# Layers 2 and 3 of a graph-network stack cut into units, with TensorE's order over three neighbouring chunks fixed by hand

## Chip, cores, metric

One core of one Trainium2 chip. The metric is the time of one execution on the device, in microseconds (us); the median of several runs is quoted. A ratio is the mean time of one kernel's runs over the mean of the other kernel's runs of the same rounds, so it is not quite the ratio of the medians quoted beside it; its 95% interval stands in brackets.

## The reference, cut

Four layers over x of 128 x 64 tokens x 256 channels, all in 32-bit floats. The change touches the last two:

```python
# layer 2: h = relu(layernorm(x))
q, k, v = split(h @ Wqkv);  s = q k^T / sqrt(256) + adj, causal
x = x + softmax(s) @ v @ Wo
# layer 3: h = relu(layernorm(x))
q, k, v = heads(h @ W);     s = q k^T / sqrt(64), -inf where adj == 0   # 4 heads of 64
x = x + softmax(s) @ v
```

(Layer 0 is a graph convolution with two batch norms, layer 1 graph convolutions and LSTMs; they take the first 1899 us and are the same in every kernel here.)

## The kernel before

The 8192 tokens are 16 chunks of 512. Each chunk's layers 2 and 3 are four functions; PE is TensorE, DVE VectorE, ACT ScalarE, POOL GpSimd. A scheduling layer takes the instructions as recorded and decides each engine's order. In the comments and views, h is the normalised input of a layer, hT its transpose, nmr the last value of the norm that h waits for (minus the mean, times rstd), tc_e and tc_f the transposes of h for layers 2 and 3, tr2 and tr3 the transposes of the softmax weights, att their copies, and o2 and o3 the outputs.

```python
        def layer2_scores(c):                               # "A"
            layernorm_relu(h, xt, f"e{c}")                  # DVE statistics, POOL rstd, ACT four h
            to_channels(hT, h, f"e{c}")                     # PE tc_e, then DVE and ACT copy hT
            nc.scalar.copy(q[:, 0, :], project_t(0, hT, wqk_sb, ...))        # PE p_q
            nc.vector.tensor_copy(q[:, 1, :], project_t(1, hT, wqk_sb, ...))
            project_v(v, hT, wvo_sb, 0, f"2_{c}")           # PE v
            ...                                             # PE scores s2, DVE mask
            softmax(s, NJ, at, f"2_{c}")                    # DVE max, POOL subtract, ACT exp, DVE
        def layer2_out(c):                                  # "B"
            transposed(at, NJ, att, f"2_{c}")               # PE tr2, ACT copies att
            ...                                             # PE o2, DVE adds it to x
        def layer3_scores(c):                               # "C"
            layernorm_relu(h, xt, f"f{c}")
            to_channels(hT, h, f"f{c}")                     # PE tc_f
            ...                                             # PE p_q, p_k, v3, scores s3, softmax
        def layer3_out(c):                                  # "D"
            transposed(at, NJ * HEADS, att, f"3_{c}")       # PE tr3, ACT and DVE copy att
            ...                                             # PE o3: 16 matmuls with 64 columns

        for c in range(NCH + 2):
            if c < NCH:             layer2_scores(c)
            if c >= 2:              layer3_out(c - 2)
            if 1 <= c <= NCH:       layer3_scores(c - 1)
            if c < NCH:             layer2_out(c)
        # ... (cut: everything else; line breaks shortened)
```

Of the kernel before, what the change touches and what calls it, by code (L numbers as in the profile page):

```python
# [19 lines left out]
def kernel(  # L20
# [23 lines left out]
    B, T, D = x.shape  # L44
# [11 lines left out]
    NCH = B * T // CH  # L56
# [12 lines left out]
    def bank(name):  # L69
        return psum.tile([P, CH], F32, tag="ps", name=name)  # L70
# [97 lines left out]
    def to_channels(dst, src, name):  # L168

        for k in range(KD):  # L170
            ps = bank(f"tc{k}_{name}")
            for j in range(NJ):
                nc.tensor.transpose(ps[:, j * P : (j + 1) * P], src[:, j, k * P : (k + 1) * P], ident)
            if k % 2 == 0:
                nc.vector.tensor_copy(dst[:, k, :], ps)  # L175
            else:
                nc.scalar.copy(dst[:, k, :], ps)
# [220 lines left out]
    with tc.tile_pool(name="w2", bufs=1) as w2p, tc.tile_pool(name="l2", bufs=2) as l2:  # L398
# [33 lines left out]
        def project_v(dst, hT, w, first, name):  # L432
            for t in range(NJ // 2):
                ps = bank(f"v_{name}_{t}").rearrange("p (j d) -> p j d", d=D)
                for i in range(2):
                    j = 2 * t + i
                    for k in range(KD):
                        nc.tensor.matmul(ps[:, i, :], hT[:, k, j * P : (j + 1) * P],  # L438
                                         w[:, k, first : first + D], start=(k == 0),
                                         stop=(k == KD - 1))  # L440
                nc.scalar.copy(dst[:, 2 * t : 2 * t + 2, :], ps)

        def project_t(m, hT, w, name):
            ps = bank(f"p{m}_{name}")
            for k in range(KD):
                nc.tensor.matmul(ps, w[:, k, m * P : (m + 1) * P], hT[:, k, :],  # L446
                                 start=(k == 0), stop=(k == KD - 1))
            return ps
# [15 lines left out]
        def transposed(src, n, dst, name):  # L464

            for b in range(n // NJ):
                ps = bank(f"tr_{name}_{b}")
                for j in range(NJ):
                    nc.tensor.transpose(ps[:, j * P : (j + 1) * P], src[:, b * NJ + j, :], ident)
                d = dst[:, b * NJ : (b + 1) * NJ, :].rearrange("p j n -> p (j n)")  # L470
                if b % 2 == 0:
                    nc.scalar.copy(d, ps)  # L472
                else:
                    nc.vector.tensor_copy(d, ps)



        parts = {}

        def layer2_scores(c):  # L480
            xt = xs[c]
            h = l2.tile([P, NJ, D], F32, tag="h", name=f"h2_{c}")
            layernorm_relu(h, xt, f"e{c}")
            hT = l2.tile([P, KD, CH], F32, tag="hT", name=f"hT2_{c}")
            to_channels(hT, h, f"e{c}")
            q = l2.tile([P, KD, CH], F32, tag="q", name=f"q2_{c}")
            nc.scalar.copy(q[:, 0, :], project_t(0, hT, wqk_sb, f"q2_{c}"))
            nc.vector.tensor_copy(q[:, 1, :], project_t(1, hT, wqk_sb, f"q2_{c}"))
            v = l2.tile([P, NJ, D], F32, tag="v", name=f"v2_{c}")
            project_v(v, hT, wvo_sb, 0, f"2_{c}")  # L490
            ps = bank(f"s2_{c}")[:, : NJ * T].rearrange("p (j t) -> p j t", t=T)
            for j in range(NJ):
                for e in range(2):
                    t = slice((2 * j + e) * T, (2 * j + e + 1) * T)
                    for k in range(KD):
                        nc.tensor.matmul(ps[e * T : (e + 1) * T, j, :], q[:, k, t], hT[:, k, t],
                                         start=(k == 0), stop=(k == KD - 1))
            s = l2.tile([P, NJ, T], F32, tag="s2", name=f"s2_{c}")
            nc.vector.scalar_tensor_tensor(s, ps, float(D) ** -0.5,
                                           mask2[:, None, :].to_broadcast([P, NJ, T]),  # L500
                                           op0=OP.mult, op1=OP.add)
            at = at2[c % 2]
            softmax(s, NJ, at, f"2_{c}")
            parts[2, c] = at, v

        def layer2_out(c):
            xt = xs[c]
            at, v = parts.pop((2, c))
            att = l2.tile([P, NJ, P], F32, tag="att2", name=f"att2_{c}")
            transposed(at, NJ, att, f"2_{c}")  # L510
            for t in range(NJ // 2):
                ps = bank(f"o2_{c}_{t}").rearrange("p (j d) -> p j d", d=D)
                for i in range(2):
                    nc.tensor.matmul(ps[:, i, :], att[:, 2 * t + i, :], v[:, 2 * t + i, :],
                                     start=True, stop=True)
                nc.vector.tensor_add(xt[:, 2 * t : 2 * t + 2, :], xt[:, 2 * t : 2 * t + 2, :], ps)

        def layer3_scores(c):
            xt = xs[c]
            h = l2.tile([P, NJ, D], F32, tag="h", name=f"h3_{c}")  # L520
            layernorm_relu(h, xt, f"f{c}")
            hT = l2.tile([P, KD, CH], F32, tag="hT", name=f"hT3_{c}")
            to_channels(hT, h, f"f{c}")
            q = l2.tile([P, KD, CH], F32, tag="q", name=f"q3_{c}")
            kk = k3[c % 2]
            for m in range(KD):
                nc.scalar.copy(q[:, m, :], project_t(m, hT, w3_sb, f"q3_{c}"))
                ps = project_t(KD + m, hT, w3_sb, f"k3_{c}").rearrange("p (b t) -> p b t", t=T)
                for e in range(2):
                    r = slice(e * HD, (e + 1) * HD)  # L530
                    nc.vector.tensor_copy(kk[r, m, :, e, :], ps[r])  # L531
            v = l2.tile([P, NJ, D], F32, tag="v", name=f"v3_{c}")
            project_v(v, hT, w3_sb, 2 * D, f"3_{c}")
            s = l2.tile([P, NJ * HEADS, T], F32, tag="s3", name=f"s3_{c}")
            for g in range(NJ // 2):
                ps = bank(f"s3_{c}_{g}").rearrange("p (j f) -> p j f", j=2)
                for i in range(2):
                    for e in range(2):
                        b = 2 * (2 * g + i) + e
                        for m in range(KD):  # L540
                            nc.tensor.matmul(
                                ps[e * T : (e + 1) * T, i, m * 2 * T : (m + 1) * 2 * T],
                                q[:, m, b * T : (b + 1) * T],
                                kk[:, m, b].rearrange("p h t -> p (h t)"),
                                start=True, stop=True)
                n = 2 * HEADS
                nc.vector.scalar_tensor_tensor(
                    s[:, g * n : (g + 1) * n, :], ps.rearrange("p j (h t) -> p (j h) t", t=T),
                    float(HD) ** -0.5, mask3[:, None, :].to_broadcast([P, n, T]),
                    op0=OP.mult, op1=OP.add)  # L550
            at = at3[c % 2]
            softmax(s, NJ * HEADS, at, f"3_{c}")
            parts[3, c] = at, v

        def layer3_out(c):
            xt = xs[c]
            at, v = parts.pop((3, c))
            att = l2.tile([P, NJ * HEADS, P], F32, tag="att3", name=f"att3_{c}")
            transposed(at, NJ * HEADS, att, f"3_{c}")
            o = l2.tile([P, NJ, D], F32, tag="o", name=f"o_{c}")  # L560
            for t in range(NJ // 2):
                ps = bank(f"o3_{c}_{t}").rearrange("p (j d) -> p j d", d=D)
                for i in range(2):
                    j = 2 * t + i
                    for hd in range(HEADS):
                        f = slice(hd * HD, (hd + 1) * HD)
                        nc.tensor.matmul(ps[:, i, f], att[:, j * HEADS + hd, :], v[:, j, f],  # L567
                                         start=True, stop=True)
                nc.vector.tensor_add(o[:, 2 * t : 2 * t + 2, :], xt[:, 2 * t : 2 * t + 2, :], ps)
            nc.sync.dma_start(outr[c], o)  # L570

        for c in range(NCH + 2):
            if c < NCH:
                layer2_scores(c)
            if c >= 2:
                layer3_out(c - 2)
            if 1 <= c <= NCH:
                layer3_scores(c - 1)
            if c < NCH:
                layer2_out(c)  # L580


# [44 lines left out]
```

## Time and profile before

| | before |
|---|---|
| median (4 runs) | 2522.52 us (2521.32 to 2523.38) |
| rounds of layers 2 and 3 | 14 from 1950.08 to 2465.89 us, 36.84 us each |
| granted TensorE clock in them | 0.92 |
| TensorE at half clock | 5.6 us a round |

A *round* runs from the end of one chunk's layer-3 scores (s3) to the next. The clock is full or half in these records, so a granted clock of 0.92 (0.924 before rounding) means that 2 x (1 - 0.924) of the time is at half. In the rounds of this trace it is at half for 3.41, 6.83 or 10.24 us at a time, and these stretches begin whole steps of 3.4133 us apart, within 0.02 us; such a step is called a *window* below. From the page's groups of instructions (line, engine, operation, tiles, shapes, count; busy us, mean ns; idle time before and what ended it), layer 3's output:

```profile
L567 PE MATMUL o<-v,att 128*128 128x64 f32 x512 | 77.1, 322 | 26.5 <-ACT att L472 26.5
```

In a round at full clock these 32 entries take 3.6 us, that is 0.11 us each from start to start; the mean duration cannot be read as a cost per matmul, as matmuls overlap.

### The profile page before, as it was taken

To read this page: it belongs to the slowest core of one execution; us is meant where nothing else is said; L and a number is where in the kernel's file an instruction comes from. 1 tells how busy PE (TensorE), PEld (TensorE's weight loads), DVE (VectorE), ACT (ScalarE), POOL (GpSimd) and SP (SyncE) were. 2 spreads that over 40 slices of the span, in tenths; PEclk is the share of its full clock that TensorE was granted. 3 is DMA by queue.
4 is the path that set the end of the run, shared out by engine and by line. 5 is a ranking of instruction groups with operands and counts; after the bars stand their busy time and mean duration, and the time that the engine had idled before them with its cause. 6 is when DMAs were issued, how large, how long until landed. Compare 5 with 4: busy or idle time off the path is not lost.

```text
span 2518.0 us, 22830 instructions
## 1 busy us (share of the span) xinstructions
PE 2293.2 (91%) x9181; PEld 1485.8 (59%) x9181; DVE 897.6 (36%) x1892; ACT 825.6 (33%) x1479; POOL 178.7 (7%) x226
## 2 busy tenths in 40 slices
PE   6989699989989989989989989998997999989996
PEld 3544255854754764764674575575575666666665
DVE  5644322222232232231232232233223555555554
ACT  4544232323323323323323333233333323333331
POOL 2100100000010010010000000000002111111110
PEclk9999899989999999999999999999998898899998
DMA  3100400000000000000000000000000000000000
GB/s 94 59 0 1 150 14 1 1 17 1 1 17 0 1 17 0 1 17 1 1 9 9 1 9 9 0 1 1 0 1 30 16 10 18 17 9 18 17 17 18
DMA packets 30122, 37.78 MB, mean 15 GB/s; under 512 B 1856, under 2 KB 27456, under 8 KB 30016
## 3 DMA queue, kind: packets, MB, share of 16 engines
q1 hardware_dynamic: 27600, 27.89, 3.5%
q0 software_dynamic: 2256, 8.40, 0.9%
q8 instruction: 72, 1.18, 0.2%
q14 instruction: 34, 0.28, 0.0%
q10 hardware_dynamic: 160, 0.03, 0.0%
HBM read 27.93 MB, written 8.39 MB: 14 GB/s over the span
## 4 chain that ended last, share of the span: by engine, by line
PE 78%; DVE 10%; POOL 4%; ACT 3%; issue 2%; DMA 2%; SPq 0%; POOLq 0%; ACTq 0%; DVEq 0%
PE g L345 31%; PE g L352 16%; PE z L250 4%; PE o L567 3%; PE z L234 3%; PE p_q L446 3%; PE agg_b L163 2%; PE v L438 2%; PE u L318 2%; PE v L309 2%; PE p_k L446 2%; DMA xt<-in_x_dram 2%; DVE at L462 2%; ACT h L153 1%; PE agg_c L163 1%
## 5 line engine op out<-in xcount | busy, mean ns | idle before, releaser
L345 PE MATMUL g<-hT,wih 128*128 128x256 f32 (+2 forms) x2496 | 818.7, 483 | 3.8 <-ACT gate L368 3.8
L345 PEld LDWEIGHTS g<-hT,wih 128*128 128x128 f32 x2496 | 468.2, 188 | 334.2 <-issue 192.5
L358 ACT ACTIVATE gate<-g,bias 128x256 f32<-128x256 f32 (+2 forms) x624 | 350.6, 562 | 747.9 <-PE g L352 616.8
L352 PE MATMUL g<-hs,whh 128*128 128x256 f32 (+2 forms) x1536 | 435.8, 437 | 0.0
L352 PEld LDWEIGHTS g<-hs,whh 128*128 128x128 f32 x1536 | 291.3, 190 | 132.2 <-issue 62.0
L362 DVE TENSOR_TENSOR cell<-cell,gate 128x256 f32<-128x256 f32 (+2 forms) x96 | 48.7, 508 | 466.6 <-ACT gate L358 466.6
L163 PE MATMUL agg_b<-adjt_bd,h 128*128 128x128 f32 x256 | 61.4, 431 | 85.3 <-ACT h L153 85.3
L392 POOL COPY hn<-hT 128x512 f32<-128x512 f32 x32 | 36.3, 1210 | 1335.7 <-DVE hT L374 1335.7
L367 DVE TENSOR_TENSOR cell<-gate,gate 128x512 f32<-128x512 f32 (+2 forms) x80 | 48.2, 602 | 224.0 <-ACT gate L358 224.0
L234 PE MATMUL z<-agg,w_sb 128*128 128x512 f32 x256 | 116.3, 608 | 8.1 <-DVE agg L227 6.9
L250 PE MATMUL z<-h,w_sb 128*128 128x512 f32 x256 | 111.6, 599 | 5.0 <-ACT h L245 5.0
L163 PEld LDWEIGHTS agg_b<-adjt_bd,h 128*128 128x128 f32 x256 | 57.3, 314 | 90.0 <-ACT h L153 89.6
L368 ACT ACTIVATE gate<-cell 128x256 f32<-128x256 f32 (+2 forms) x176 | 89.9, 511 | 50.0 <-DVE cell L367 41.0
L567 PE MATMUL o<-v,att 128*128 128x64 f32 x512 | 77.1, 322 | 26.5 <-ACT att L472 26.5
L374 DVE TENSOR_TENSOR hT<-gate,gate 128x512 f32<-128x512 f32 (+2 forms) x80 | 48.1, 601 | 127.2 <-PE g L345 100.5
L567 PEld LDWEIGHTS o<-v,att 128*128 128x128 f32 x512 | 74.7, 235 | 29.9 <-ACT att L472 29.8
L250 PEld LDWEIGHTS z<-h,w_sb 128*128 128x128 f32 x256 | 49.2, 193 | 67.4 <-issue 57.2
L234 PEld LDWEIGHTS z<-agg,w_sb 128*128 128x128 f32 x256 | 48.0, 193 | 66.2 <-issue 47.8
L531 DVE COPY k<-p_k 64x512 f32<-64x512 f32 x64 | 44.1, 689 | 102.9 <-PE p_k L446 102.5
L446 PE MATMUL p_q<-hT,w_sb 128*128 128x512 f32 x128 | 73.9, 708 | 2.3 <-DVE hT L175 2.3
L153 ACT ACTIVATE h<-xs,nmr_b,rstd_b 128x256 f32<-128x256 f32 x64 | 33.2, 588 | 127.0 <-DVE nmr_b L151 127.0
L371 DVE TENSOR_TENSOR hs<-gate,gate 128x256 f32<-128x256 f32 (+2 forms) x96 | 47.8, 497 | 72.8 <-ACT gate L368 44.6
(151 smaller groups left out, 2406.2 us busy)
## 6 DMA issues: line engine op xcount, KB each, us to landing
xt<-in_x_dram SPq DMA_DIRECT2D x32, 512.0 KB, 3.9
out_dram<-o SPq DMA_DIRECT2D x16, 512.0 KB, 2.9
wih<-in_wih_t_dram POOLq DMA_DIRECT2D x4, 1024.0 KB, 13.1
whh<-in_whh_t_dram POOLq DMA_DIRECT2D x3, 1024.0 KB, 17.9
w_sb<-in_w_dram SPq DMA_DIRECT2D x1, 768.0 KB, 4.4
wqkv_sb<-in_wqkv_dram SPq DMA_DIRECT2D x1, 768.0 KB, 4.4
w_sb<-in_w1t_dram POOLq DMA_DIRECT2D x1, 512.0 KB, 4.6
w_sb<-in_w2t_dram POOLq DMA_DIRECT2D x1, 512.0 KB, 5.7
```

Of the source, the lines that this page charges most:

```text
L153: nc.scalar.activation(dst[:, j, :], src[:, j, :], AF.Relu, bias=nmr[:, j : j + 1], scale=rstd[:, j : j + 1])
L163: nc.tensor.matmul(ps[:, j * P : (j + 1) * P], src[:, j, k * P : (k + 1) * P], mat, start=True, stop=True)
L234: nc.tensor.matmul(ps, w1_sb[:, k, m * P : (m + 1) * P], agg[:, k, :], start=(k == 0), stop=(k == KD - 1))
L250: nc.tensor.matmul(ps, w2_sb[:, k, m * P : (m + 1) * P], h1[:, k, :], start=(k == 0), stop=(k == KH - 1))
L309: nc.tensor.matmul(ps, wg0_sb[:, k, m * P : (m + 1) * P], agg[:, k, :], start=False, stop=(k == KD - 1))
L318: nc.tensor.matmul(ps[:, i, :], v[:, k, j * P : (j + 1) * P], wg1_sb[:, k, :], start=(k == 0), stop=(k == KD - 1))
L345: nc.tensor.matmul(banks[q][:, :n].rearrange("p (j w e) -> p j w e", w=nw, e=2), wi[:, k, o], hv[:, k, :, cols, :], start=(k == 0), stop=( ...
L352: nc.tensor.matmul(banks[q][:, :n], wh[:, k, o], hs[:, k, :n], start=False, stop=(k == KD - 1))
L358: nc.scalar.activation(g[q], banks[q][:, :n], AF.Tanh if q == 2 else AF.Sigmoid, bias=bs[:, q * KD + c : q * KD + c + 1])
L368: nc.scalar.activation(g[2], cell[c], AF.Tanh)
L446: nc.tensor.matmul(ps, w[:, k, m * P : (m + 1) * P], hT[:, k, :], start=(k == 0), stop=(k == KD - 1))
L567: nc.tensor.matmul(ps[:, i, f], att[:, j * HEADS + hd, :], v[:, j, f], start=True, stop=True)
```

## The change

Intent: no engine's work changes; TensorE's waits between a transpose and the use of its copied result are to be filled with another chunk's work. The four functions become generators that stop after each unit, and a table fixes TensorE's order.

```diff
             to_channels(hT, h, f"e{c}")
+            yield
...(a yield after every unit: norm, q, v, scores; transposed weights, output)
-        for c in range(NCH + 2):
-            if c < NCH:
-                layer2_scores(c)
-            if c >= 2:
-                layer3_out(c - 2)
-            if 1 <= c <= NCH:
-                layer3_scores(c - 1)
-            if c < NCH:
-                layer2_out(c)
+        stages = {"A": layer2_scores, "B": layer2_out, "C": layer3_scores, "D": layer3_out}
+        ROUND = (("A", 0), ("A", 0), ("A", 0), ("D", -2), ("C", -1), ("D", -2), ("C", -1), ("B", 0),
+                 ("C", -1), ("C", -1), ("A", 1), ("B", 0))
...
+        with tc.manual_schedule(engines={mybir.EngineType.PE}):
+            unit("A", 0)
+            for c in range(NCH + 2):
+                for stage, d in ROUND:
+                    unit(stage, c + d)
```

More of the change, by code (lines that the diff above doesn't have):

```diff
@@ L488, in layer2_scores @@
             nc.vector.tensor_copy(q[:, 1, :], project_t(1, hT, wqk_sb, f"q2_{c}"))
+            yield
             v = l2.tile([P, NJ, D], F32, tag="v", name=f"v2_{c}")
             project_v(v, hT, wvo_sb, 0, f"2_{c}")
+            yield
             ps = bank(f"s2_{c}")[:, : NJ * T].rearrange("p (j t) -> p j t", t=T)
@@ L504, in layer2_scores @@
             parts[2, c] = at, v
+            yield
         def layer2_out(c):
@@ L510, in layer2_out @@
             transposed(at, NJ, att, f"2_{c}")
+            yield
             for t in range(NJ // 2):
@@ L516, in layer2_out @@
                 nc.vector.tensor_add(xt[:, 2 * t : 2 * t + 2, :], xt[:, 2 * t : 2 * t + 2, :], ps)
+            yield
         def layer3_scores(c):
@@ L523, in layer3_scores @@
             to_channels(hT, h, f"f{c}")
+            yield
             q = l2.tile([P, KD, CH], F32, tag="q", name=f"q3_{c}")
@@ L531, in layer3_scores @@
                     nc.vector.tensor_copy(kk[r, m, :, e, :], ps[r])
+            yield
             v = l2.tile([P, NJ, D], F32, tag="v", name=f"v3_{c}")
             project_v(v, hT, w3_sb, 2 * D, f"3_{c}")
+            yield
             s = l2.tile([P, NJ * HEADS, T], F32, tag="s3", name=f"s3_{c}")
@@ L553, in layer3_scores @@
             parts[3, c] = at, v
+            yield
         def layer3_out(c):
@@ L559, in layer3_out @@
             transposed(at, NJ * HEADS, att, f"3_{c}")
+            yield
             o = l2.tile([P, NJ, D], F32, tag="o", name=f"o_{c}")
@@ L570, in layer3_out, with unit @@
             nc.sync.dma_start(outr[c], o)
-        for c in range(NCH + 2):
-            if c < NCH:
-                layer2_scores(c)
-            if c >= 2:
-                layer3_out(c - 2)
-            if 1 <= c <= NCH:
-                layer3_scores(c - 1)
-            if c < NCH:
-                layer2_out(c)
+            yield
+        stages = {"A": layer2_scores, "B": layer2_out, "C": layer3_scores, "D": layer3_out}
+        ROUND = (("A", 0), ("A", 0), ("A", 0), ("D", -2), ("C", -1), ("D", -2), ("C", -1), ("B", 0),
+                 ("C", -1), ("C", -1), ("A", 1), ("B", 0))
+        units = {}
+        def unit(stage, c):
+            if 0 <= c < NCH:
+                if (stage, c) not in units:
+                    units[stage, c] = stages[stage](c)
+                next(units[stage, c])
+        with tc.manual_schedule(engines={mybir.EngineType.PE}):
[3 more added lines that the diff above has]
+                    unit(stage, c + d)
 def kernel(**inputs):
```

## The prediction

> **What bounds the kernel now.** I read the page's slices first, then what TensorE waited for, then one round of the last stage instruction by instruction. From the page of the kernel before:
>
> ```profile
> PE   6989699989989989989989989998997999989996
> PEclk9999899989999999999999999999998898899998
> ```
>
> TensorE (PE) is busy nearly everywhere, and the granted clock is worst in the last quarter (1899 to 2518 us), where layers 2 and 3 run: the only part that the diff touches. There 14 near-equal rounds run from 1950.08 to 2465.89, 515.8 us, 36.84 us each. PE's waits in that stretch:
>
> ```profile
> PE o L567 <- ACT att L472: 26.5, 14, 2.2
> PE p_q L446 <- DVE hT L175: 11.2, 17, 0.7
> PE o L514 <- ACT att L472: 9.4, 14, 0.7
> ```
>
> Only 47.1 us in 14 rounds, 3.4 us a round, is shown as waiting. The rest of the loss is clock. Two whole rounds and two stretches of the first, by the view of windows (the column after POOL busy is the granted clock):
>
> ```profile
> 2101.24:2138.60 37.36, 34.04 (x198) 24.50 (x196) 20.64 (x44) 12.22 (x22) 5.06 (x6) 0.91 0.05 15
> 2213.40:2248.06 34.66, 30.84 (x198) 22.21 (x197) 20.56 (x44) 12.22 (x22) 5.06 (x6) 1.00 0.05 16
> ...
> 2117.42:2120.83 3.41, 2.57 (x23) 2.57 (x24) 2.64 (x6) 3.06 (x7) 0.61 (x1) 1.00 0.00 0
> 2120.83:2127.66 6.83, 6.83 (x23) 4.95 (x23) 2.28 (x5) 0.69 (x2) 0.00 (x0) 0.50 0.23 77
> ```
>
> A round at full clock takes 34.66 us, one that falls to half clock for 6.83 us takes 37.36; the mean round loses 36.84 - 34.66 = 2.2 us to the clock. Now the middle of the round that starts at 2101.24 (end of layer 3's scores), all engines:
>
> ```profile
> 2113.22 1.20 PE L496 MATMUL s<-hT,q 128*64 128x64 f32 x32
> 2114.16 0.16 DVE L151 SCALAR_TENSOR_TENSOR nmr_f<-mv_f,rstd_f 128x4 f32<-128x4 f32 x1 [1.23 <-POOL rstd_f L81]
> 2114.35 1.97 PE L469 MATMUL tr<-ident,at 128*128 128x128 f32 x16
> 2114.41 1.09 ACT L153 ACTIVATE h<-xs,nmr_f,rstd_f 128x256 f32<-128x256 f32 x2 [2.17 <-DVE nmr_f L151]
> ...
> 2115.80 1.04 POOL L81 TENSOR_TENSOR rstd_e<-rstd_e,mhalf 128x4 f32<-128x4 f32 x1
> 2115.88 1.09 ACT L153 ACTIVATE h<-xs,nmr_f,rstd_f 128x256 f32<-128x256 f32 x2
> ...
> 2117.91 0.61 POOL L454 TENSOR_TENSOR s<-s,mx 128x256 f32<-128x256 f32 x1 [1.06 <-DVE mx L453]
> 2118.26 2.00 PE L567 MATMUL o<-v,att 128*128 128x64 f32 x16 [1.95 <-ACT att L472]
> 2118.56 0.42 ACT L455 ACTIVATE s<-s 128x256 f32<-128x256 f32 x1 [0.35 <-POOL s L454]
> ```
>
> The four normalised tiles h of layer 3's next chunk are ready only at 2116.97, 15.7 us into the round, and the exponential of layer 2's softmax starts 17.3 us in. That is no matter before, as PE comes to h only after layer 3's output, at 2122.83 (21.6 us in). Layer 3's output waits 1.95 us for its transposed weights, and the clock falls in its middle.
>
> [...] the granted-clock records of before fall to 0.5 for 3.41, 6.83 or 10.24 us. But windows need not be idle: one with 2.57 us of layer 3's output (64-column matmuls) lowered it, and three with nothing but that output at half clock did not restore it, while full windows of 512-column projections always did. [...] a window with only 1.8 us of transposes at 2226.6 did not lower the clock. [...]
>
> **The change part by part.** No instruction is added or removed; PE's order within a round becomes: h-transposes of layer 2 (tc_e), output of layer 2 (o2), p_q, v, scores s2, weight transposes of layer 3 (tr3), h-transposes of layer 3 (tc_f), output of layer 3 (o3), q/k projections, weight transposes of layer 2 (tr2), v3, scores s3. The scheduler re-orders the other engines to suit; I read their built order.
>
> Removed: tr2 followed at once by o2 (0.67 us wait) now has v3 and s3 between; tc_e followed at once by p_q (0.69) has o2 between; tc_f to q/k (0.5 at full clock) has o3 between; tr3 to o3 (1.95) has tc_f between. 3.8 us a round, the gain that was meant: 14 x 3.8 = 53 us, and more if the clock stays up.
>
> Added: tc_f comes right after tr3. When is h ready? I walk the round from t = 0 at the end of s3 with durations of the round shown (start-to-start where they overlap).
> - PE at full clock: tc_e 0.9, o2 1.83 to 2.73, p_q 3.53 to 6.26, v 3.55 to 9.81, s2 1.13 to 10.94, tr3 1.82 to **12.76**. Here PE wants h.
> - VectorE: mask of s3 to 0.80, hT copy (now ahead) to 1.52, row maximum to 2.77; GpSimd subtract 2.92 to 4.83; ScalarE exp to 5.94; VectorE sum 5.96, reciprocal, q copy, then the two 1.2 us products to 10.6; the last statistics of layer 3's norm end at 11.41 (they ended at 11.37 before). GpSimd's rstd takes 1.39 with its hand-overs, nmr at 12.96 (before: 12.92). So h's chain does not move, but its user comes 9 us earlier.
> - ScalarE's built order is h, h, weight copy, h, **exp of layer 2's softmax**, weight copy, h. The exp waits for GpSimd, which does rstd of layer 2's next norm first: VectorE reaches s2's mask at 13.83, ends the norm's statistics at 14.5, GpSimd rstd 14.66 to 16.02, subtract 16.1 to 16.7, exp to 17.2, copy to 17.6, the fourth h to **18.1**. In all middle rounds the built order is the same.
> - So PE stands from 12.76 to 18.1 (three transposes in between), o3 can start at 18.7 instead of 17.0. At full clock: 18.7 + o3 3.63 + q/k 6.97 + tr2 0.5 + v3 3.55 + s3 1.95 = **35.3 us**, against 34.66 before: the four short waits became one long one behind the same chain.
>
> Clock: PE does almost nothing for 5.3 us, so at least one window of 3.41 us is nearly empty in every round, and the clock falls between 15.0 and 18.4, before o3 starts. o3 does not restore it, so all of it runs at half: +3.6 us; the last transposes +0.5; then q/k until a window without o3 has passed, 2.6 to 6.0 us (mean 4.3, half lost: +2.1). Together +6.3: a round of about **41.6 us**, +4.8 over 36.84. Times 14: +67 us. The first round and the tail keep their waits (6.5 and 9.2 us behind the last softmaxes), +-2 us.
>
> **The rivals.** (1) What the author wants: all 3.8 us a round go, PE never stands, the clock stays at 1.00: a round of 30.9, 14 x -5.9 = -83 us, 2440 us. For it: every pair of transpose and use gets other work in between. Against it: h's first tile cannot be there before 13.2, and tr3 ends at 12.76. (2) The long wait is there, but the clock recovers during o3 or falls late, as in the trace's single-window cases: 35.3 + about 2.5 = 37.8, +1.0 a round, +14 us, 2537: the same. (3) Full clock throughout: 35.3, that is 14 x -1.5 = -21 us, 2502; it needs an empty window not to count, and the before-trace shows such windows lowering the clock every time. (4) Banks or transfers as a new bound: eight banks still suffice (tr3 4, tc_f 2, s2 and v one each before o3), and the output store takes 2.9 us of some 37; I give them nothing.
>
> **Range and chances.** The walk gives 2523 + 67 = 2590. I shade it to 2582, as (2) is half as likely as the main line. The low end, 2530, is rival (2); the high end, 2606, is +5.9 a round: four windows of half clock (13.65 us, half lost, where the main line has 12.6 us) and a chain 0.6 us longer. Slower by over 2% begins at 2573.5: 0.60. Same: 0.34, rivals (2) and (3) and a milder clock. Faster by over 2%: 0.06, if the walk misreads the chain.
>
> **What would show it.** Right: the waits named att and hT nearly vanish from PE's list, and one new line stands first, tc_f waiting for ScalarE's h, about 4 to 5 us a round; o3 takes about 7.2 us instead of 4.8; the granted clock in the stage falls from about 0.92 to near 0.83; rounds of 40 to 42 us. Wrong: the fourth h is earlier than 17 us into the round, or the clock is restored while o3 runs, or rounds are under 37 us.

(35.3 us of the walk and 6.3 us of clock make the 41.6 us. The clock's terms are estimates from windows of the trace before: three with 0.00, 0.22 and 0.56 us of matmuls (1895.55, 2468.99, 2496.29) were each followed by half clock; three with the output alone at half clock (1967.23, 2192.51, 2339.28) by half clock again, two with projections alone (2199.34, 2346.11) by full. The walk assumes that ScalarE and VectorE keep their built order. In the round at 2111.67 of the trace after they did: the norm (nmr_f) was done at 2124.34, yet ScalarE idled 1.25 us before the exponential and made the fourth h only behind it; VectorE idled 0.65 us for the next norm ahead of a copy of weights whose transposes had ended at 2124.42. TensorE's work stands there in the order of the table.)

## The result, and the profile after

| | before | after |
|---|---|---|
| median (4 runs each) | 2522.52 us | **2565.32 us** (2565.2 to 2567.33) |
| ratio | | 1.0172 [1.0154, 1.019] |
| mean of 14 rounds | 36.84 us | 40.06 us |
| half clock a round | 5.6 us | 12.7 us |

1.7% slower: within 2%, though clear of noise. The 14 rounds account for 14 x 3.22 = 45 us of the 45.3 us between the two profiled spans. The page's slices:

```profile
PE   6999699989989989989989989989989898988996
PEclk9999799999999999999999999999998888878888
```

TensorE looks as busy as before (91% of the span), which says nothing: its matmuls last longer at half clock (the output's 32 entries 6.7 us in the round below, 3.5 us at full clock in the first experiment). What TensorE waited for in layers 2 and 3 (us in total, times, longest):

```profile
PE tc_f L173 <- ACT h L153: 51.9, 57, 2.6
PE tr L469 <- DVE at L462: 20.6, 3, 9.2
...
PE p_q L446 <- DVE hT L175: 0.8, 2, 0.4
```

The 47.1 us of waits on att and hT in the rounds are gone, and one line of 51.9 us has taken their place: 3.7 us a round on the tiles h of layer 3. The round that starts at 2111.67, TensorE and ScalarE:

```profile
2122.45 1.97 PE L469 MATMUL tr<-ident,at 128*128 128x128 f32 x16
2124.44 1.09 ACT L153 ACTIVATE h<-xs,nmr_f,rstd_f 128x256 f32<-128x256 f32 x2 [2.43 <-DVE nmr_f L151]
...
2125.91 0.60 ACT L153 ACTIVATE h<-xs,nmr_f,rstd_f 128x256 f32<-128x256 f32 x1
...
2127.75 0.42 ACT L455 ACTIVATE s<-s 128x256 f32<-128x256 f32 x1 [1.25 <-POOL s L454]
2128.07 0.57 ACT L472 COPY att<-tr 128x512 f32<-128x512 f32 x1
2128.54 0.60 ACT L153 ACTIVATE h<-xs,nmr_f,rstd_f 128x256 f32<-128x256 f32 x1
...
2129.19 1.33 PE L173 MATMUL tc_f<-ident,h 128*128 128x128 f32 x5 [2.31 <-ACT h L153]
2130.31 6.93 PE L579 MATMUL o<-v,att 128*128 128x64 f32 x32
```

Layer 3's weight transposes (tr) end 12.6 us into the round; ScalarE makes two h, one h, then stands until the exponential (L455) can run at 2127.75, and only then makes the fourth h, done 17.5 us in. TensorE gets five transposes at 2129.19 and starts layer 3's output at 2130.31; that output takes 6.7 us up to the next instruction. The view of windows shows the clock in it (the column after POOL busy is the granted clock):

```profile
2125.26:2128.67 3.41, 0.82 (x3) 0.28 (x2) 2.75 (x8) 2.16 (x6) 1.86 (x3) 1.00 0.01 2
2128.67:2142.32 13.65, 13.13 (x44) 10.03 (x45) 2.99 (x6) 3.61 (x7) 0.00 (x0) 0.50 0.11 38
2142.32:2145.74 3.42, 3.42 (x10) 1.51 (x9) 1.38 (x2) 0.59 (x1) 0.00 (x0) 1.00 0.00 0
```

One window of 3.41 us with 0.82 us of matmuls, then four windows at half clock, through the whole output and into the projections.

### The profile page after: what moved, and what is told of

It reads as the page before. It is cut to its first block, busy times and chain, and to the rows that moved or that the text cites. A ratio compares the mean times of both kernels' runs of the same rounds, so it can differ in the third digit from the quotient of the medians.

```text
span 2563.3 us, 22860 instructions
## 1 busy us (share of the span) xinstructions
PE 2333.2 (91%) x9181; PEld 1520.2 (59%) x9181; DVE 895.1 (35%) x1892; ACT 825.7 (32%) x1479; POOL 178.1 (7%) x226
## 4 chain that ended last, share of the span: by engine, by line
PE 78%; DVE 10%; POOL 5%; ACT 3%; issue 2%; DMA 2%; SPq 0%; POOLq 0%; ACTq 0%; DVEq 0%
PE g L345 31%; PE g L352 16%; PE z L250 4%; PE o L579 4%; PE p_q L446 3%; PE z L234 3%; PE agg_b L163 2%; PE p_k L446 2%; PE u L318 2%; PE v L438 2%; PE v L309 2%; DMA xt<-in_x_dram 2%; DVE at L462 1%; POOL s L454 1%; ACT h L153 1%
## 5 line engine op out<-in xcount | busy, mean ns | idle before, releaser
L579 PEld LDWEIGHTS o<-v,att 128*128 128x128 f32 x512 | 104.7, 316 | 0.0
L579 PE MATMUL o<-v,att 128*128 128x64 f32 x512 | 104.4, 400 | 0.0
L446 PE MATMUL p_q<-hT,w_sb 128*128 128x512 f32 x128 | 84.3, 793 | 0.6 <-DVE hT L175 0.3
L173 PE MATMUL tc_f<-ident,h 128*128 128x128 f32 x128 | 34.4, 374 | 51.9 <-ACT h L153 51.9
L535 ACT COPY q<-p_q 128x512 f32<-128x512 f32 x32 | 18.8, 586 | 176.1 <-PE p_q L446 176.1
```

Source lines behind the costliest of these rows:

```text
L446: nc.tensor.matmul(ps, w[:, k, m * P : (m + 1) * P], hT[:, k, :], start=(k == 0), stop=(k == KD - 1))
L579: nc.tensor.matmul(ps[:, i, f], att[:, j * HEADS + hd, :], v[:, j, f], start=True, stop=True)
```

## The experiments

A wait and a clock that falls are mixed in the result. My theory: the change moved the use of h ahead of a chain over DVE, POOL and ACT that ends 17 to 18 us into the round in both kernels; the wait alone costs nothing against before, and the loss is clock. Rivals: the wait itself is the loss; or ScalarE's order (the fourth h behind an exponential) is all of it. Round means and half clock come from each run's trace, the before columns from the same chip.

| run | median us | before us | ratio | round us | half clock us a round |
|---|---|---|---|---|---|
| changed kernel | 2565.32 | 2522.52 | 1.0172 | 40.06 | 12.7 |
| e2_fill5 | 2495.64 | 2528.78 | 0.9867 | 34.48 | 0 |
| e3_before_fill2 | 2492.05 | 2528.78 | 0.9855 | 34.62 | 0 |
| e1_output_before_tc_f | 2509.26 | 2528.78 | 0.9924 | 35.77 | 6.8 |
| e7_softmax2_later | 2528.84 | 2520.29 | 1.0033 | 37.42 | 10.0 |
| e5_norm_first | 2449.73 | 2528.78 | 0.9685 | 31.43 | 0 |
| e6_old_order_norm_first | 2510.47 | 2520.29 | 0.9962 | 35.87 | 3.7 |
| e4_lag3 | 2481.12 | 2520.29 | 0.9843 | 33.80 | 3.4 |
| e9_lag3_norm_first_q_act | 2470.11 | 2520.29 | 0.9798 | 33.27 | 2.9 |
| e10_lag3_s2_between | **2431.93** | 2521.44 | 0.9637 | 30.37 | 0.2 |

All outputs are right. Each ran 4 times; no ratio's interval reaches further than 0.0033 from its ratio.

### Useless matmuls in the wait, changed kernel

```diff
+        def fill(n, name):
+            ps = bank(f"fill_{name}")
+            for i in range(n):
+                nc.tensor.matmul(ps, w3_sb[:, i % KD, :P], w3_sb[:, i % KD, :CH], start=True, stop=True)
...
             transposed(at, NJ * HEADS, att, f"3_{c}")
+            fill(5, f"3_{c}")
             yield
```

> The changed kernel with five useless 128x512 matmuls (about 0.86 us each, result never read) between layer 3's weight transposes and the h transposes: they lie in the wait for h and keep PE busy, so the wait stays and the half clock should go. Theory (of the round's 40.1 us, about 5.5 us are half clock): granted clock near 1.00 in the rounds, layer 3's output 3.6 us instead of 6.7, rounds of 34.6 us, total 2490 to 2500 us (some 7 us of it added in the tail, where the filler is not hidden). Rival (the loss is the wait alone): 2565 us or a little more.

Measured 2495.64 us, rounds of 34.48 us, as expected. One round of its trace:

```profile
2099.89 1.97 PE L469 MATMUL tr<-ident,at 128*128 128x128 f32 x16
2101.69 4.46 PE L482 MATMUL fill<-w_sb 128*128 128x512 f32 x10
2105.99 0.49 PE L173 MATMUL tc_f<-ident,h 128*128 128x128 f32 x3
2106.64 0.77 PE L173 MATMUL tc_f<-ident,h 128*128 128x128 f32 x5 [0.16 <-ACT h L153]
2107.24 3.68 PE L585 MATMUL o<-v,att 128*128 128x64 f32 x32
```

Over 14 rounds the view of windows gives full clock (1.00 after POOL busy):

```profile
1950.97:2433.68 482.71, 480.54 (x2887) 336.92 (x2885) 285.95 (x607) 167.40 (x304) 69.05 (x82) 1.00 0.05 16
```

The last h comes at the same place: the transposes resume 17.5 us after the round's start at 2089.12. Yet the output now takes 3.5 us in place of 6.7, and the round is 5.58 us shorter. So of the changed kernel's 40.06 us, 5.58 are clock (14 x 5.58 = 78 us, 3.0% of its time), shown by giving TensorE something to do and changing nothing that the result needs. (The scheduler answered the filler with one small move on ScalarE and one on VectorE, both after the last h.)

### Useless matmuls in the wait, kernel before

The same helper, `fill(2, f"3_{c}")` after layer 3's weight transposes, in the 1.95 us wait.

> The kernel before with two useless 128x512 matmuls between layer 3's weight transposes and its output, in the 1.95 us wait. Theory (the round before loses 36.84 - 34.66 = 2.2 us to the clock): rounds of 34.7 us, total 2490 to 2500 us. Rival (half clock is set by the kind of matmul in layer 3's output, not by the wait): 2522 to 2528 us, clock unchanged.

Measured 2492.05 us, rounds of 34.62 us, no half clock:

```profile
1950.77:2435.50 484.73, 455.57 (x2803) 320.60 (x2802) 287.55 (x607) 168.67 (x304) 69.40 (x82) 1.00 0.05 16
```

So the kernel before lost 36.84 - 34.62 = 2.2 us a round to the clock. **With the clock full, the two kernels have rounds of 34.48 and 34.62 us.** Of the +3.22 us a round, the clock is 5.58 - 2.22 = +3.36, the order itself -0.14: the four short waits that the change removed came back as one. The +3.36 is less sharp than it looks: single runs of the kernel before range from 2515.45 us (granted clock 0.958 over the whole kernel) to 2531.27 us (0.950), which is 1.1 us a round, and 2.22 is that of the profiled run. The -0.14 compares two kernels at full clock on one chip.

### Layer 3's output ahead of the transposes of h

```diff
-        ROUND = (("A", 0), ("A", 0), ("A", 0), ("D", -2), ("C", -1), ("D", -2), ("C", -1), ("B", 0),
+        ROUND = (("A", 0), ("A", 0), ("A", 0), ("D", -2), ("D", -2), ("C", -1), ("C", -1), ("B", 0),
```

> The changed kernel with one part of PE's new order undone: layer 3's output stands before the transposes of h again; the other moves stay. Theory (the chain from the scores over VectorE, GpSimd and ScalarE to the last att copy at about 17.6 us and the last h at about 17.5 us sets the round, PE's order only decides where it waits and how much runs at half clock): output waits for att instead, rounds of 36 to 37 us, total 2510 to 2530 us, no gain over before although three of before's four short waits stay away. Rival (each short wait taken away is worth its length): 1.9 us a round less than before, 2497 us or lower.

Measured 2509.26 us, rounds of 35.77 us: 0.7 us and 0.2 us under the theory's ranges, 12 us above the rival's. It is a gain over before that is clear of noise (0.9924 [0.9907, 0.994]), where the theory expected none: 1.07 us a round, and the rival's 1.9 did not come either, so neither text holds as it stands. The waits:

```profile
PE o L579 <- ACT att L472: 30.9, 27, 1.9
```

Before's waits for hT and for the weights of layer 2 are not in the rounds' list any more, and TensorE waits instead 2.2 us a round for the weights of layer 3, in two pieces. (The transposes tc_f and the q/k projections are still neighbours here, as before; in before's rounds that wait shows only in the three at full clock, 0.50 us each.) Half clock is 6.8 us a round, 1.2 more than before. How much of the round the chain sets is not shown by this run. This run differs from the changed kernel's order in one exchange, tc_f against o3, and is 56 us faster (ratios to before 0.9924 and 1.0172): the loss comes with that pair, whose exchange joins the waits into one long one.

### Layer 3's norm recorded first

```diff
             layernorm_relu(h, xt, f"f{c}")
+            yield
             hT = l2.tile([P, KD, CH], F32, tag="hT", name=f"hT3_{c}")
...
-        ROUND = (("A", 0), ("A", 0), ("A", 0), ("D", -2), ("C", -1), ("D", -2), ("C", -1), ("B", 0),
-                 ("C", -1), ("C", -1), ("A", 1), ("B", 0))
+        ROUND = (("C", -1), ("A", 0), ("A", 0), ("A", 0), ("D", -2), ("C", -1), ("D", -2), ("C", -1),
+                 ("B", 0), ("C", -1), ("C", -1), ("A", 1), ("B", 0))
```

> The changed kernel with layer 3's norm made a unit of its own that is recorded ahead of layer 2's q, so that ScalarE gets all four h before the exponential of layer 2's softmax; PE's order is the same. Theory (the fourth h stands behind that exponential): last h at about 15.3 us instead of 17.5, output from 16 us, rounds of 37.5 to 38.5 us (the clock still falls), total 2530 to 2545 us. Rival (h is late because of its own chain, not because of ScalarE's order): 2560 us or more.

Measured **2449.73 us**, far below either theory: rounds of 31.43 us at full clock. TensorE's order is that of the changed kernel; only the other engines' orders differ. In a round that starts at 2110.66:

```profile
2122.24 0.16 DVE L151 SCALAR_TENSOR_TENSOR nmr_f<-mv_f,rstd_f 128x4 f32<-128x4 f32 x1 [0.97 <-POOL rstd_f L81]
...
2122.50 2.08 ACT L153 ACTIVATE h<-xs,nmr_f,rstd_f 128x256 f32<-128x256 f32 x4 [1.51 <-DVE nmr_f L151]
...
2124.21 1.18 PE L173 MATMUL tc_f<-ident,h 128*128 128x128 f32 x8
```

All four h are done at 2124.58, 13.9 us in. I had foreseen ScalarE's order and missed VectorE's: with the norm recorded first, the last statistics run before the two 1.2 us softmax products, so the norm is ready 11.6 us in and not 12.5. That is 0.9 us of the 3.6 by which the last h comes earlier; the rest is ScalarE's order, which now makes the four h one behind the other, ahead of the copies of weights and of the exponential. TensorE, held 0.7 us by a copy of q, arrives just as the h do. The clock stays full (1.00 from 1952 to 2390 us), and 8.6 us a round are gone.

### The fourth h ahead of the exponential, nothing else

```diff
                         nc.tensor.matmul(ps[e * T : (e + 1) * T, j, :], q[:, k, t], hT[:, k, t],
                                          start=(k == 0), stop=(k == KD - 1))
+            yield
             s = l2.tile([P, NJ, T], F32, tag="s2", name=f"s2_{c}")
...
-        ROUND = (("A", 0), ("A", 0), ("A", 0), ("D", -2), ("C", -1), ("D", -2), ("C", -1), ("B", 0),
+        ROUND = (("A", 0), ("A", 0), ("A", 0), ("D", -2), ("C", -1), ("A", 0), ("D", -2), ("C", -1),
+                 ("B", 0),
```

> The changed kernel with one edit: layer 2's mask and softmax are a unit of their own, recorded after the transposes of h. PE's, VectorE's and GpSimd's orders stay; on ScalarE the fourth h now stands before layer 2's exponential (h, h, att, h, att, h, exp). This parts the two things that the run with the norm first did together (ScalarE's order, and layer 3's statistics ahead of the softmax products). Theory (waiting behind the exponential costs the fourth h 1.7 us, and the long wait still empties a window): fourth transposes at about 15.9 us into the round instead of 17.5, half clock stays at 3 to 4 windows, rounds of 38 to 38.6 us, 2535 to 2545 us. Rival (the exponential in front of the fourth h is the whole loss): below 2500 us.

Measured 2528.84 us, rounds of 37.42 us. In a round that starts at 2100.60:

```profile
2116.45 1.33 PE L173 MATMUL tc_f<-ident,h 128*128 128x128 f32 x5 [0.64 <-ACT h L153]
2117.57 6.93 PE L580 MATMUL o<-v,att 128*128 128x64 f32 x32
```

The last transposes come 15.85 us in, as expected (17.5 in the changed kernel), but the output still takes 6.7 us: the wait for h is shorter (2.1 us in four pieces, where the changed kernel has 3.8 in the round shown), and the clock is still at half when the output runs. The gain was larger than I expected, 2.6 us a round in place of 1.5 to 2.1, as the half clock also shrank by 2.7 us. The rival (the exponential in front of the fourth h is the whole loss) fails by 29 us: with the h ahead of it, the kernel is still no faster than before. That does not clear the rest of ScalarE's order: two copies of weights still stand between the h here, and none in the run with the norm first. Its last h is done 13.9 us into the round, here 15.8: 0.9 us of that is VectorE's order (the statistics ahead of the products), 1.0 us is these copies. TensorE also comes to h 1.0 us later there, as it waits for q. No run parts these three. (In VectorE's order one copy moved a few places, after the last h.)

### The norm first under the old order

Units, norm first, but TensorE's order as before, fixed by hand: `ROUND = A, C(norm), A, A, A, D, D, C, C, C, C, B, B` with offsets 0 for A and B, -1 for C, -2 for D; the first unit of A is not taken a round ahead.

> The units with PE's order of the kernel before (output of layer 3 ahead of the transposes of h, weight transposes followed at once by their output), fixed by hand, and layer 3's norm recorded ahead of layer 2's q. Theory (the norm first pays only together with the new PE order, since in the old one layer 3's output waits for att, not for h): 2510 to 2530 us, as before. Rival (the norm first is the whole gain of the run with 2449.7 us): 2450 to 2470 us.

Measured 2510.47 us (0.9962), rounds of 35.87 us. TensorE waited 24.3 us for att, 12.7 for hT and 9.4 for att of layer 2, nearly before's list. So the early norm is worth 0.4% under the old order and the new order costs 1.7% with the late norm, but the two together give 3.2%. I read that as each removing what hides the other. Even the 0.4% is clock: the rounds of this run without half clock take 34.4 to 34.7 us, as before's 34.66.

### A lag of three chunks

Layer 3's output three chunks behind, ahead of the transposes of h; more TensorE work lies before h is needed.

```diff
+        ROUND = (("A", 0), ("D", -3), ("A", 0), ("A", 0), ("D", -3), ("C", -1), ("C", -1), ("B", 0),
+                 ("C", -1), ("C", -1), ("A", 1), ("B", 0))
...
-        at3 = [w2p.tile([P, NJ * HEADS, P], F32, name=f"at3_{i}") for i in range(2)]
+        at3 = [w2p.tile([P, NJ * HEADS, P], F32, name=f"at3_{i}") for i in range(3)]
```

(also v of layer 3 in its own three buffers, one buffer each for s3, att3 and o to make room, and a loop to NCH + 3)

> The changed kernel with layer 3's output three chunks behind instead of two, and ahead of the transposes of h: round p_q, weight transposes of layer 3, v, s2, output of layer 3, transposes of h; three buffers of its softmax's result and of v, one each of three smaller tiles to make room. Theory (what counts is how much PE work that waits for nothing lies between layer 2's output and h's transposes: 14 us in place of 10): PE reaches h at 16.2 us, where h is ready, no long wait, full clock, rounds of 30 to 30.5 us, 2420 to 2440 us. Rival (the chain moves with the extra att copies and h is late again): a wait of over 2 us at h, half clock, over 2500 us.

Measured 2481.12 us, rounds of 33.80 us: a gain, but both texts miss. In the steady rounds TensorE did not wait for h, as the theory said; the wait came one step later:

```profile
PE p_q L446 <- DVE hT L175: 34.0, 16, 2.6
```

The transposes were done, but VectorE's copy of them stood behind the sum of layer 2's softmax, which stood behind the exponential.

The same with the norm first and layer 2's second q copy on ScalarE (`nc.scalar.copy(q[:, 1, :], ...)`):

> The run before this one with the norm of layer 3 recorded first and the second half of layer 2's q copied by ScalarE. Theory (PE has no wait left in the rounds): rounds of 30 us, within 10 us of the run with the lag of three, 2415 to 2435 us; both beat the kernel before and the run with the norm first. Rival (VectorE or ScalarE becomes the bound): rounds over 31 us.

Measured 2470.11 us, rounds of 33.27 us, a miss too: the same wait, up to 2.1 us a round.

### Layer 2's scores between the transposes of h and their use

```diff
+        ROUND = (("C", -1), ("A", 0), ("D", -3), ("A", 0), ("D", -3), ("C", -1), ("A", 0), ("C", -1),
+                 ("B", 0), ("C", -1), ("C", -1), ("A", 1), ("B", 0))
```

(lag of three, norm first, q copied as in the changed kernel)

> Layer 3's output three chunks behind, its norm recorded first, and layer 2's scores moved between the transposes of h and the q/k projections: the two kernels with a lag of three waited 2.1 to 2.6 us there for VectorE's copy of hT, which stood behind the work on layer 2's scores. Theory (each transpose needs other PE work ahead of its use, and VectorE's copy must not stand behind a chain): no wait over 0.7 us in the rounds, full clock, rounds of 30 to 30.6 us, 2420 to 2435 us, faster than the run with the norm first (2449.7 us) and than all others. Rival (another chain takes its place at once): rounds over 31.4 us, 2450 us or more.

Measured **2431.93 us**, 0.9637 [0.9604, 0.967], rounds of 30.37 us: as expected, and faster than both kernels. (Only the first round has a wait over 0.7 us, 2.7 us for h, and a window at half clock.) Against the first run with a lag of three it has the early norm too, so what the place of layer 2's scores is worth by itself is not shown. Its view of windows over the rounds, and what is left of that wait:

```profile
1951.00:2376.00 425.00, 419.05 (x2697) 307.79 (x2695) 278.02 (x604) 167.89 (x302) 69.39 (x82) 1.00 0.05 17
```

```profile
PE p_q L446 <- DVE hT L175: 2.7, 13, 0.4
```

TensorE is busy 98.6% of these 425 us at full clock.

## Why the prediction was right or wrong, step by step

- **The exchange of waits: right.** The short waits on att and hT vanished, one line, tc_f waiting for ScalarE's h, stands first. It lists 3.7 us a round; I said 4 to 5. ScalarE's order with the exponential before the fourth h was the one read from the build.
- **The place of the fourth h: right in kind, predicted 0.6 us too late.** Predicted 18.1 us into the round, measured 17.5. Some 0.45 us of that is VectorE's run up to the norm (nmr predicted at 12.96, measured at 12.51): I added the copies and the maximum at their durations, and they overlap more.
- **The round at full clock: predicted 35.3, measured 34.48** (with the filler). This term was over by 0.8 us.
- **The clock: predicted +6.3 us a round, measured 5.58.** In the round shown it is 6.3: compared with the filled kernel, transposes +0.5, output 6.72 in place of 3.52 (+3.2), projections 9.56 in place of 6.92 (+2.6). But rounds run from 39.2 to 40.85 us as they slide against the windows, and four of the 14 have three windows of half clock (10.24 us), not four (13.65). I took the mean over places of the window as if each were as likely. Nor does a stretch of 5.3 us always hold a whole window of 3.41 us, as I wrote it did nearly; that the clock fell in each of the 14 rounds is measured.
- **Sum:** 41.6 predicted, 40.06 measured; the walk's 2590 is 25 us too high, and 14 x (0.8 + 0.7) = 21 us of that are these two terms. The range held. The chances did not lead with what came: 0.60 for slower by over 2%, against +1.7% measured; both mis-sized terms point the same way. The shading from 2590 to 2582 came nearer by luck: it was made for rival (2), a clock that recovers during o3, and that did not happen.
- **Rival (1)**, no wait at all and 2440 us, was what the idea could yield, but not in this form; the last run reaches 2431.93 us, with the norm as one more unit, a lag of three and more buffers. **Rival (3)**, the wait at full clock and 2502 us, did not come by itself; the filler run forced it and measured 2495.64 us, 7.6 us of it extra tail.
- **"o3 does not restore the clock":** held in every round: each of the 14 half-clock stretches ends 1.8 to 5.1 us after the output, in the q/k projections. That projections restore it held too.

What stays open: what in a window decides whether the next is at half clock. In the trace before, a window with 1.67 us of half-clock output and 1.74 us of transposes was followed by full clock (2158.4 us), one with 1.34 and 1.84 us, later in a half-clock stretch, was not (2195.9 us). One with 2.57 us of output at full clock was followed by half clock (2117.42); one with 1.80 us of transposes alone stayed at full clock and was followed by full clock, as was one with 3.41 us of transposes at half clock:

```profile
2226.64:2230.05 3.41, 1.80 (x16) 1.56 (x15) 1.83 (x8) 3.24 (x7) 1.28 (x3) 1.00 0.02 5
2475.81:2479.22 3.41, 3.41 (x17) 3.30 (x17) 0.87 (x3) 1.72 (x4) 1.28 (x2) 0.50 0.00 0
```

No run here parts the explanations.

## What to carry to other kernels

Removing a wait pays only if the next thing in that engine's order is ready (here it came 3.7 us a round late); walk the chain that feeds it over the other engines, in their built orders, before fixing one engine's order by hand. A few short waits can be cheaper than one long one of about the same sum: here they cost 2.2 us of clock a round, the long one 5.6, with rounds of 34.62 and 34.48 us at full clock. A few useless matmuls in the wait told in one run each how much of the loss was clock. When TensorE's order is fixed, also record early what feeds it, since the scheduler orders the other engines by what was recorded first as well (2449.73 us with the norm recorded first, 2565.32 without, TensorE's order the same).
